# A two-layer graph network with fast matrix products: the statistics of u and h laid between the inner copies, adj's T4 and the logit weights moved in the first batch, and the first softmax's exponentials put to other steps

## The chip, the cores and the metric

The kernel runs on one core of a Trainium2 chip. The metric is the time of one execution on the device in microseconds (us), the median of several runs. A core has TensorE (PE, matrix products; PEld is its loading of weights), VectorE (DVE), ScalarE (ACT), GpSimd (POOL) and the queue SP, which here only issues transfers (DMAs). Each engine works through its own instructions in the order in which the program wrote them. [...]

## The reference

```python
# x: 16 x 1024 x 512, adj: 1024 x 1024, all float32
# layer 0
h = maximum(layernorm(x), 0)
x = x + (adj @ h) @ W0 + bias
# layer 1 (graph attention)
u = maximum(layernorm(x), 0)
hw = u @ W1
e = leaky_relu(s1[:, :, None] + s2[:, None, :], 0.2) * adj   # s1 = hw @ a1, s2 = hw @ a2
att = softmax(e, axis=2)
x = x + elu(att @ hw + beta * hw)
```

The kernel works out att @ u first and multiplies by W1 afterwards; beta is added on the diagonal of att. So s1 and s2 come straight from u: u times (W1 @ a1) and u times (W1 @ a2). These two vectors are the "logit weights".

## The kernel before

All 16 batches go through layer 0, and then all 16 through layer 1. Every large product is made with seven block products instead of eight (Strassen's scheme in Winograd's form). `PRODUCTS` (line 44) names them p1 to p7 with their two operands; S1 to S4 are sums of blocks of the left operand, T1 to T4 of the right one. `ReadA` (line 121) takes the finished products out of the accumulators (PSUM): ScalarE copies p1, p6, p5 and p4, VectorE adds p2, p7 and p3 and then makes the sums S1, S2, S3 for the product with W.

One batch of layer 0 has two parts. The first is adj times h ("y"). In batch 0 it is made by the plain `products_a` in 14 steps, in the others by `products_a2` (line 193) in 28 steps, k = 0 to 27. There four of the seven products (p1, p5, p3, p4) are themselves made with seven inner products, written in the order r1, r4, r5, r6, r2, r7, r3. Inner products alternate with quarters of the plain ones: p1 with p2 (steps 0 to 6), p5 with p6 (7 to 13), p3 with p7 (14 to 20), and p4 with the first product of the second part (21 to 27). Between inner products small copies and sums have to be made before the next may overwrite its accumulator: ScalarE copies r1, r5 and r7 into the tiles y_p1t, in_p (the sums' last quarter) and so on, VectorE adds to r6 (`step`, line 229). The operands' inner block sums are made ahead of that by `inner_left` (line 384). The second part is y times W0 ("po"), by `Weighted` (line 304), in 14 steps of two per product. Its results are added to the tiles xr, which hold x as the residual; GpSimd adds the bias to them (`add_bias`).

Between these steps everything else is laid by hand. A plan is a table of step numbers with functions that are called after the step; `beside` (line 520) calls them. Every engine's instructions and every transfer are kept in the order of writing (`InOrder`, line 103), which is also why each record of the profile has line 111. In batch b of layer 0 these stand beside the products:

- for batch b - 1, after its residual is complete: `keep` stores x + layer 0 for layer 1; `stats` are ScalarE's sums for the layer norm of u (a pass for the mean, one for the variance), `relu` makes u in place, `logits` multiplies it on VectorE with the two logit weights, `sums` makes u's block sums, `store` writes u away (`plan_out`, line 1071). `load_res` then loads the next residual into the same tiles. Full-size outputs that nobody needs, of `stats` and of `logits`, go into a half of the tile of S1 of u (`junk`, line 610), the half chosen by q.
- for batch b + 1: `h_stats` and `h_relu` make h out of x, `h_sums` its block sums (`plan_norm_a`, `plan_norm_b`, lines 1098 and 1105).
- for layer 1's first softmax, ahead of time: in batches 5 to 12 one eighth each of the masked logits e is made and stored (`EARLY_B`, line 1143); batch 15 reloads these (R), takes their exponentials with transposes (E), makes the sums over rows (S, s), the diagonal (D, d) and the block sums T1 to T3 (`FIRST_A`, `FIRST_B`, lines 1151 and 1155).

From batch 1 on, steps 0 and 1 of the second part's plan are called in the first part, after its steps 23 and 26 (line 1201).

In batch 0 `plan_first` (line 1051) also transposes adj, makes its block sums T1 to T4 and their inner sums, and the two logit weights are worked out in steps 3 and 5 of the second part.

Of the kernel before, what the change touches and what calls it, by code (L numbers as in the profile page):

```python
# [61 lines left out]
def kernel(  # L62
# [58 lines left out]
    class ReadA:  # L121
# [1 line left out]


        def __init__(self, name):
            self.name, self.c, self.s = name, {}, {}

        def block(self, n, p):
            if n not in self.c:
# [3 lines left out]
        def __call__(self, prod, p, ps):  # L133
            s = self.s
            if prod == "p1":
                act.copy(self.block("C11", p), ps)
            elif prod == "p2":
                c11 = self.block("C11", p)
                add(c11, ps, c11)
            elif prod == "p6":  # L140
                act.copy(self.block("C12", p), ps)
            elif prod == "p5":
                act.copy(self.block("C22", p), ps)
            elif prod == "p7":
                c22 = self.block("C22", p)
                add(c22, ps, c22)
            elif prod == "p3":
                if not s:
                    for k in ("S1", "S2", "S4"):
                        s[k] = b4.tile([P, 2, 512], F32, tag="b4", name=f"{self.name}_{k}")  # L150
                c11, c12, c22 = (self.block(n, p) for n in ("C11", "C12", "C22"))
                s1, s2 = s["S1"][:, p, :], s["S2"][:, p, :]
                add(c12, ps, c12)
                add(s1, c12, c22)
                add(s2, s1, c11, ALU.subtract)
                add(c12, c11, c12, ALU.subtract)
            else:
                act.copy(self.block("C21", p), ps)
                self.last(p)

        def last(self, p):
            add(self.s["S4"][:, p, :], self.block("C21", p), self.s["S2"][:, p, :], ALU.subtract)
# [30 lines left out]
    def products_a2(name, a_blk, b_blk, inner, weighted, after):  # L193


        read = ReadA(name)
        banks = {}
        by_name = {p[0]: (n, *p[1:]) for n, p in enumerate(PRODUCTS)}

# [74 lines left out]
        for two, one in (("p1", "p2"), ("p5", "p6"), ("p3", "p7")):  # L274
            inn, pla = inner_steps(two), plain_steps(one)
            for m in range(7):
                inn[m]()
                pla[m if m < 4 else m + 1]()
                if m == 3:
                    pla[4]()  # L280
                    if one != "p2":
                        reads(one, 0)
                elif m == 5:
                    reads(two, 0)
                    if one == "p2":
                        reads(one, 0)
                elif m == 6:
                    for prod in (two, one) if one == "p2" else (one, two):
                        reads(prod, 1)
                after(k + m)  # L290
            k += 7
        inn = inner_steps("p4")
        steps = iter(weighted.steps(0, read.c["C11"]))
        for m in range(7):
            inn[m]()
            if m > 4:
                read.last(m - 5)
            next(steps)()
            if m == 3:
                next(steps)()  # L300
            after(k + m)
        return read.left()

# [258 lines left out]
    def layer0_b(b, plan):  # L562
        left = lefts.pop(b)
        if b in weighted:
            weighted.pop(b).rest(1, left, beside(plan))
        else:
            Weighted(f"po{b}", w0_c, partial(to_residual, b)).rest(0, left, beside(plan))

    x1d = {}
    ud = {}  # L570
# [480 lines left out]
    def plan_first():  # L1051
        return {
            1: [(h_sums, 0, 0), (transpose_adj, 0, 1), (transpose_adj, 1, 0), (h_sums, 0, 1)]
            + [(transpose_adj, 1, 1), (adj_sum, "T1"), (adj_sum, "T2")],
            4: [(adj_sum, "T3")], 5: [(adj_sum, "T4")], 6: [(w_sums, w0_c)],
            7: [(inner_right, "p1", 0), (inner_right, "p1", 1)],
            8: [(inner_right, "p5", 0), (inner_right, "p5", 1)], 9: [(inner_right, "p3", 0)],
            10: [(inner_right, "p4", 0)],
        }
# [4 lines left out]
            plan.setdefault(k, []).append(tuple(step))  # L1064
        return plan

    def in_fourteen(plan):

        return merged(*({k // 2 if k > 0 else k: v} for k, v in plan.items()))

    def plan_out(o, b):

        return steps(
            (-1, o.keep, 0, 1), (-1, o.keep, 1, 0), (-1, o.keep, 1, 1), (-1, o.stats, 0, 1, 1),
            (0, o.stats, 1, 0, 0), (1, o.stats, 1, 0, 1), (2, o.stats, 1, 1, 0),
            (3, o.relu, 0, 0), (4, o.stats, 1, 1, 1), (5, o.relu, 1, 0), (6, o.relu, 0, 1),
            (8, o.relu, 1, 1),
            (0, inner_left, b, "p3"), (1, inner_left, b, "p4"),
            (5, o.logits, 0, 0, 0), (7, o.logits, 0, 0, 1),
            (8, o.logits, 1, 0, 0), (9, o.logits, 1, 0, 1),  # L1080
            (10, o.sums, 0, 0), (11, o.sums, 0, 1), (11, o.store, 0),
            (12, o.logits, 0, 1, 0), (13, o.logits, 0, 1, 1), (13, load_res, b, 0, 0),
            (14, o.logits, 1, 1, 0), (15, o.logits, 1, 1, 1), (15, load_res, b, 1, 0),
            (16, o.sums, 1, 0), (17, o.sums, 1, 1), (17, o.store, 1),
            (19, load_res, b, 0, 1), (21, load_res, b, 1, 1),
        )

    def plan_bias(b):
# [8 lines left out]

    def plan_norm_a(b):
        return steps(
            (9, h_stats, b, 0, 0), (10, h_stats, b, 0, 1), (12, h_stats, b, 1, 0),  # L1100
            (13, h_stats, b, 1, 1), (14, h_relu, b, 0), (15, load_x, b, 2), (16, h_relu, b, 1),
            (17, load_x, b, 3),
        )

    def plan_norm_b(b):
        plan = steps(
            (0, h_stats, b, 2, 0), (1, h_stats, b, 2, 1), (2, h_stats, b, 3, 0),
            (3, h_stats, b, 3, 1), (4, h_relu, b, 2), (6, h_relu, b, 3), (8, h_sums, b, 0),
            (10, h_sums, b, 1),
        )  # L1110
        if b + 1 < B:
            plan = merged(plan, steps((7, load_x, b + 1, 0), (7, load_x, b + 1, 1)))
        return merged(plan, steps((12, inner_left, b, "p1"), (13, inner_left, b, "p5")))

    def plan_softmax(order, s):
        names = {
# [12 lines left out]
        for n in ("T1", "T2", "T3", "T4"):  # L1129
# [13 lines left out]
    EARLY_B = {  # L1143
        4: {10: "L"},
        **{
            5 + g: {4: f"e{g}", 8: f"M{g}", 12: f"K{g}" + {3: " X", 7: " x"}.get(g, "")}
            for g in range(NCH)
        },
        13: {9: "N n"},
    }  # L1150
    FIRST_A = {
        1: "R0", 4: "R1", 7: "B E0 R2", 9: "E1 R3", 12: "E2 R4", 14: "E3", 15: "S b", 17: "R5",
        21: "R6", 22: "E4",
    }
    FIRST_B = {
        0: "E5", 1: "D R7", 2: "E6", 4: "E7 s", 7: "T1a", 8: "T1b", 10: "d", 11: "T2a",
        12: "T2b", 13: "T3a T3b",
    }
    LOADS_U = {5: ("U00",), 7: ("U01",), 9: ("U10", "U11"), 11: ("S2",), 13: ("S1", "S4")}


# [2 lines left out]
    for b in range(B):  # L1164
        plans = [plan_out(out_of, b)] if b else []
        plans_b = [plan_bias(b)]
        if b + 1 < B:
            plans.append(plan_norm_a(b + 1))
            out_of = LayerOut(b)
            plans_b += [  # L1170
                plan_norm_b(b + 1), plan_softmax(EARLY_B.get(b, {}), sms[0]),
                steps(
                    (11, out_of.stats, 0, 0, 0), (12, out_of.stats, 0, 0, 1),
                    (13, out_of.stats, 0, 1, 0), (12, out_of.keep, 0, 0),
                ),
            ]
        else:
            plans.append(plan_softmax(FIRST_A, sms[0]))
            plans.append({
                22: [(load_u, 0, ("U00", "U01"))], 25: [(load_u, 0, ("U10", "U11"))],  # L1180
            })
            plans_b += [
                plan_softmax(FIRST_B, sms[0]), plan_softmax(LOGITS_B, sms[1]),
                steps((3, load_u, 0, ("S2", "S1", "S4"))),
            ]
        if 0 < b <= G:
            plans.append({23: [(store_mask, b - 1)]})
        if b == 0:
            plan_b = merged(
                {  # L1190
                    1: [(inner_right, "p3", 1)], 2: [(inner_right, "p4", 1)],
                    3: [(logit_weights, 0)], 5: [(logit_weights, 1)],
                },
                *plans_b,
            )
            layer0_a(b, merged(plan_first(), in_fourteen(merged(*plans))))
        else:
            if b == 1:
                plans.append({-1: [(logit_weights_back, 0), (logit_weights_back, 1)]})
            plan_b = merged(*plans_b)  # L1200
            plans.append({k: plan_b.pop(i) for k, i in ((23, 0), (26, 1))})
            layer0_a2(b, merged(*plans))
        layer0_b(b, plan_b)


# [5 lines left out]
    for b in range(B):  # L1211
# [4 lines left out]
        plans.append({7 + i: [(load_x1, b, nh, q)] for i, (nh, q) in enumerate(halves)})  # L1216
        plan_b = {}
        if b == 0:
            plans.append({12: [(w_sums, w1_c)]})
        if b + 1 < B:  # L1220
            plans.append(plan_softmax(SOFTMAX_A, sms[b + 1]))
            plans.append({k: [(load_u, b + 1, n)] for k, n in LOADS_U.items()})
# [50 lines left out]
```

## Time and profile before

| | us |
|---|---|
| median of the runs (2347.12 to 2350.27) | 2349.37 |
| the profiled execution | 2345.13 |
| its span, first to last instruction | 2343.3 |
| PE, DVE, ACT, POOL busy | 2294.7, 1782.8, 1496.8, 582.9 |
| layer 0, batch 0 (from 11.0, the first instructions before it) | 87.5 |
| layer 0, batch 1 | 69.5 |
| layer 0, batch 7 | 71.1 |
| layer 0, batch 15 | 84.6 |
| layer 1, batch 0 | 72.2 |
| mean granted TensorE clock | 0.995 |

A row of the profile names the engine, the operation, the tile written and the tiles read without their numbers: y_p5t is batch b's small tile of p5, y_Y, y_X, y_W are accumulators of the first part, y_C its blocks read out, po_Y those of the second part; xr is the residual and later u; hS and in_p are sums of h; uS with s is the logits' output, uS with mv_u that of u's statistics; er is an eighth of e loaded back, and pT its transpose. "[1.15 <-ACT y_C]" behind a row means that the engine stood idle for 1.15 us before it, until ScalarE's writing of y_C released it. A batch's length is taken from the start of its p1 to the next.

### The profile page before, as it was taken

Reading aid. Unit: us, or ns where it says so; the run is one execution under the profiler, and the core shown is the slowest. Engines: PE = TensorE matmul, PEld = TensorE weight load, DVE = VectorE, ACT = ScalarE, POOL = GpSimd, SP = SyncE. Lnnn points to the kernel's source line nnn. Section 1 sums busy time; section 2 is a strip of 40 time slices with the busy share of each in tenths; the row PEclk is TensorE's granted clock in tenths of the full one; section 3 lists DMA queues with packets and bytes.
Section 4 is the critical chain, followed back from the end, with each engine's and each line's share of the span. In section 5 each row is a group of like instructions: output and inputs, shape, how many; then the busy total and the mean of one; then the engine's idle time right before and its main releaser. Section 6 shows DMA issues by size and latency. Waiting matters only on the chain.

```text
span 2343.3 us, 28480 instructions
## 1 busy us (share of the span) xinstructions
PE 2294.7 (98%) x7984; PEld 1511.0 (64%) x7984; DVE 1782.8 (76%) x3932; ACT 1496.8 (64%) x4025; POOL 582.9 (25%) x680
## 2 busy tenths in 40 slices
PE   9899999999999999999899999999999999999998
PEld 5677777777667777677655666556665566655665
DVE  4887777787777787877877787777877778777774
ACT  4565767665767666666357676666766677667743
POOL 1333223333223333232102221122211222102220
PEclk9999999999999999999999999999999999999999
DMA  6254544454543554433754556555565545555541
GB/s 229 64 189 153 171 151 131 153 189 145 171 150 124 168 189 145 163 120 123 245 184 155 166 178 206 173 178 166 189 211 173 186 159 167 179 182 166 175 128 44
DMA packets 207247, 383.15 MB, mean 164 GB/s; under 512 B 80240, under 2 KB 88432, under 8 KB 207088
## 3 DMA queue, kind: packets, MB, share of 16 engines
q1 hardware_dynamic: 206768, 380.81, 49.8%
q8 instruction: 63, 1.03, 0.2%
q14 instruction: 96, 0.79, 0.1%
q10 hardware_dynamic: 320, 0.52, 0.1%
HBM read 251.92 MB, written 133.50 MB: 164 GB/s over the span
## 4 chain that ended last, share of the span: by engine, by line
PE 60%; ACT 14%; DVE 13%; DMA 7%; issue 4%; SPq 2%; POOL 0%; ACTq 0%; DVEq 0%; POOLq 0%
PE z_Y L111 12%; PE y_Y L111 9%; PE pq_Y L111 6%; PE z_X L111 6%; PE po_Y L111 6%; ACT uS L111 5%; PE z_W L111 4%; PE pq_X L111 3%; PE y_X L111 3%; DVE e L111 2%; PE po_X L111 2%; DMA md<-mx 2%; ACT e L111 2%; PE po_W L111 2%; DVE hS L111 2%
## 5 line engine op out<-in xcount | busy, mean ns | idle before, releaser
L111 POOL TENSOR_TENSOR x<-x,r 128x512 f32<-128x512 f32 x120 | 226.0, 1894 | 874.7 <-DVE x L111 432.1
L111 ACT ACTIVATE e<-e,nm 128x256 f32<-128x256 f32 x480 | 237.4, 498 | 162.3 <-DVE nm L111 162.3
L111 DVE CUSTOM_DVE_ANT_0 e<-e,mask 128x256 f32<-128x256 f32 x512 | 233.2, 508 | 66.2 <-DMA mask<-maskd 34.8
L111 POOL TENSOR_TENSOR xr<-xr,bias_bc 128x512 f32<-128x512 f32 x128 | 168.2, 1336 | 269.0 <-DMA xr<-in_x_dram 182.8
L111 PE MATMUL z_Y<-pT,ul_U 128*128 128x512 f32 x512 | 224.9, 592 | 0.0
L111 ACT ACTIVATE e<-s2b,s1b 128x256 f32<-128x256 f32 x512 | 215.1, 506 | 9.0 <-DMA s2b<-s2d 9.0
L111 DVE STREAM_TRANSPOSE pT<-e 128x512 f32<-128x512 f32 x240 | 155.6, 686 | 67.4 <-ACT e L111 67.4
L111 PE MATMUL po_Y<-w_c,y_C 128*128 128x256 f32 x768 | 191.5, 384 | 3.8 <-DVE xr L111 3.8
L111 PE MATMUL pq_Y<-w_c,z_C 128*128 128x256 f32 x768 | 175.4, 380 | 0.6
L111 PEld LDWEIGHTS z_Y<-pT,ul_U 128*128 128x128 f32 x512 | 97.3, 190 | 115.6 <-issue 111.7
L111 DVE CUSTOM_DVE_ANT_0 uS<-xr,v_bc 128x512 f32<-128x512 f32 x240 | 165.7, 691 | 6.2
L111 ACT ACTIVATE r<-z,rs 128x256 f32<-128x256 f32 x192 | 95.7, 499 | 110.9 <-DVE z L111 110.9
L111 PEld LDWEIGHTS pq_Y<-w_c,z_C 128*128 128x128 f32 x768 | 145.1, 190 | 30.4 <-issue 7.7
L111 PEld LDWEIGHTS po_Y<-w_c,y_C 128*128 128x128 f32 x768 | 148.2, 193 | 25.5 <-DVE xr L111 4.2
L111 PE MATMUL y_Y<-adjT_B,h 128*128 128x512 f32 (+1 forms) x332 | 149.7, 554 | 1.6 <-ACT adjT_B L111 1.6
L111 ACT ACTIVATE uS<-xr 128x512 f32<-128x512 f32 x120 | 75.1, 626 | 119.0 <-DVE xr L111 102.7
L111 PE MATMUL y_Y<-adjT_T,hS 128*128 128x512 f32 x256 | 128.9, 599 | 9.8 <-ACT y_C L111 9.8
L111 PE MATMUL y_W<-adjT_B,h 128*128 128x512 f32 x256 | 127.2, 592 | 0.0
L111 ACT ACTIVATE h<-x,nb_h,r_h 128x512 f32<-128x512 f32 (+1 forms) x132 | 98.2, 793 | 44.6 <-POOL nb_h L111 43.4
L111 DVE TENSOR_TENSOR xr<-po_Y,xr 128x512 f32<-128x512 f32 x128 | 87.4, 684 | 41.6 <-PE po_Y L111 38.8
L111 ACT COPY z_C<-z_Y 128x512 f32<-128x512 f32 x96 | 55.5, 578 | 96.9 <-PE z_Y L111 96.9
L111 PE MATMUL po_X<-w_c,y_S 128*128 128x256 f32 x512 | 115.7, 379 | 0.0
(202 smaller groups left out, 4952.8 us busy)
## 6 DMA issues: line engine op xcount, KB each, us to landing
mask<-maskd SPq DMA_DIRECT2D x128, 512.0 KB
x<-in_x_dram SPq DMA_DIRECT2D x64, 512.0 KB
xr<-in_x_dram SPq DMA_DIRECT2D x256, 128.0 KB
x1d<-xr SPq DMA_DIRECT2D x64, 512.0 KB
ul_U<-ud_U SPq DMA_DIRECT2D x64, 512.0 KB
x<-x1d SPq DMA_DIRECT2D x64, 512.0 KB
out_dram<-x SPq DMA_DIRECT2D x252, 128.0 KB
ud_U<-xr SPq DMA_DIRECT2D x60, 512.0 KB
```

The lines of the kernel that those rows point to most:

```text
L111: return lambda *args, **kwargs: tc.keep_in_program_order(f(*args, **kwargs))
```

## The change

- Batch 0: T4 of adj is made after step 4 with T3, not after 5, and the logit weights after step 5 of the first part, not after 3 and 5 of the second; they are read back at step 0 of the second part, no longer at the start of batch 1. The plans that stand beside are no longer put to half their step numbers but to 4 plus half, at most 13. Its second part takes the order `A12_LATE`.
- Every later batch: a new order of `stats`, `relu`, `logits`, `sums`, stores and loads (`plan_out`); the h statistics and relus of batch b + 1 go from steps 9 to 16 to steps 14 to 19, and in the second part two steps later; `inner_left` of p5 goes into step 2 of the first part. The stats of u (0, 1, 0) are now made in the next batch.
- `products_a2`: both halves of p2 are read after step 7, no longer after 5 and 6. The sums S3 are made after p4's fourth inner product, not with p3's read.
- The early masks are loaded, used and stored at steps 0, 3 and 6 of the second part, no longer at 4, 8 and 12.
- Batch 15: the exponentials and reloads are at other steps, T3 is made in layer 1's first batch.

```diff
@@ class ReadA
-                add(c12, c11, c12, ALU.subtract)
+                if self.s3_now:
+                    self.s3(p)
...
+        def s3(self, p):
+            c11, c12 = self.block("C11", p), self.block("C12", p)
+            add(c12, c11, c12, ALU.subtract)
@@ products_a2
+        read.s3_now = False
...
-                if m == 3:
+                if m == 0 and two == "p5":
+                    reads("p2", 0)
+                    reads("p2", 1)
+                elif m == 3:
                     pla[4]()
                     if one != "p2":
                         reads(one, 0)
                 elif m == 5:
                     reads(two, 0)
-                    if one == "p2":
-                        reads(one, 0)
                 elif m == 6:
-                    for prod in (two, one) if one == "p2" else (one, two):
+                    for prod in (two,) if one == "p2" else (one, two):
                         reads(prod, 1)
...
             if m == 3:
                 next(steps)()
+                read.s3(0)
+                read.s3(1)
@@ layer0_b
-            Weighted(f"po{b}", w0_c, partial(to_residual, b)).rest(0, left, beside(plan))
+            Weighted(f"po{b}", w0_c, partial(to_residual, b), A12_LATE).rest(
+                0, left, beside(plan)
+            )
@@ plan_first
-            4: [(adj_sum, "T3")], 5: [(adj_sum, "T4")], 6: [(w_sums, w0_c)],
+            4: [(adj_sum, "T3"), (adj_sum, "T4")],
+            5: [(logit_weights, 0), (logit_weights, 1)], 6: [(w_sums, w0_c)],
@@
-    def in_fourteen(plan):
-
-        return merged(*({k // 2 if k > 0 else k: v} for k, v in plan.items()))
+    def at_end(plan):
+
+        return merged(*({min(4 + k // 2, 13): v} for k, v in plan.items()))
@@ plan_out
-            (-1, o.keep, 0, 1), (-1, o.keep, 1, 0), (-1, o.keep, 1, 1), (-1, o.stats, 0, 1, 1),
-            (0, o.stats, 1, 0, 0), (1, o.stats, 1, 0, 1), (2, o.stats, 1, 1, 0),
-            (3, o.relu, 0, 0), (4, o.stats, 1, 1, 1), (5, o.relu, 1, 0), (6, o.relu, 0, 1),
-            (8, o.relu, 1, 1),
-            (0, inner_left, b, "p3"), (1, inner_left, b, "p4"),
-            (5, o.logits, 0, 0, 0), (7, o.logits, 0, 0, 1),
-            (8, o.logits, 1, 0, 0), (9, o.logits, 1, 0, 1),
-            (10, o.sums, 0, 0), (11, o.sums, 0, 1), (11, o.store, 0),
-            (12, o.logits, 0, 1, 0), (13, o.logits, 0, 1, 1), (13, load_res, b, 0, 0),
-            (14, o.logits, 1, 1, 0), (15, o.logits, 1, 1, 1), (15, load_res, b, 1, 0),
-            (16, o.sums, 1, 0), (17, o.sums, 1, 1), (17, o.store, 1),
-            (19, load_res, b, 0, 1), (21, load_res, b, 1, 1),
+            (-1, o.keep, 0, 1), (-1, o.keep, 1, 0), (-1, o.keep, 1, 1), (0, o.stats, 0, 1, 0),
+            (1, o.stats, 0, 1, 1), (2, o.stats, 1, 0, 0), (3, o.stats, 1, 0, 1),
+            (4, o.relu, 0, 0), (7, o.relu, 0, 1), (8, o.stats, 1, 1, 0), (9, o.stats, 1, 1, 1),
+            (10, o.relu, 1, 0), (11, o.relu, 1, 1),
+            (0, inner_left, b, "p3"), (1, inner_left, b, "p4"), (2, inner_left, b, "p5"),
+            (5, o.logits, 0, 0, 0), (6, o.logits, 0, 0, 1), (8, o.logits, 0, 1, 0),
+            (9, o.logits, 0, 1, 1), (11, o.logits, 1, 0, 0), (12, o.logits, 1, 0, 1),
+            (13, o.sums, 0, 0), (14, o.sums, 0, 1), (14, o.store, 0), (15, o.logits, 1, 1, 0),
+            (16, o.logits, 1, 1, 1), (16, load_res, b, 0, 0), (17, load_res, b, 0, 1),
+            (17, o.sums, 1, 0), (18, o.sums, 1, 1), (18, o.store, 1),
+            (21, load_res, b, 1, 0), (22, load_res, b, 1, 1),
@@ plan_norm_a
-            (9, h_stats, b, 0, 0), (10, h_stats, b, 0, 1), (12, h_stats, b, 1, 0),
-            (13, h_stats, b, 1, 1), (14, h_relu, b, 0), (15, load_x, b, 2), (16, h_relu, b, 1),
-            (17, load_x, b, 3),
+            (14, h_stats, b, 0, 0), (15, h_stats, b, 0, 1), (16, h_stats, b, 1, 0),
+            (17, h_stats, b, 1, 1), (18, h_relu, b, 0), (19, load_x, b, 2), (19, h_relu, b, 1),
+            (20, load_x, b, 3),
@@ plan_norm_b
-            (0, h_stats, b, 2, 0), (1, h_stats, b, 2, 1), (2, h_stats, b, 3, 0),
-            (3, h_stats, b, 3, 1), (4, h_relu, b, 2), (6, h_relu, b, 3), (8, h_sums, b, 0),
-            (10, h_sums, b, 1),
+            (2, h_stats, b, 2, 0), (3, h_stats, b, 2, 1), (4, h_stats, b, 3, 0),
+            (5, h_stats, b, 3, 1), (6, h_relu, b, 2), (7, h_relu, b, 3), (8, h_sums, b, 0),
+            (10, h_sums, b, 1), (12, inner_left, b, "p1"),
         )
         if b + 1 < B:
-            plan = merged(plan, steps((7, load_x, b + 1, 0), (7, load_x, b + 1, 1)))
-        return merged(plan, steps((12, inner_left, b, "p1"), (13, inner_left, b, "p5")))
+            plan = merged(plan, steps((8, load_x, b + 1, 0), (8, load_x, b + 1, 1)))
+        return plan
@@ EARLY_B
-            5 + g: {4: f"e{g}", 8: f"M{g}", 12: f"K{g}" + {3: " X", 7: " x"}.get(g, "")}
+            5 + g: {0: f"e{g}", 3: f"M{g}", 6: f"K{g}" + {3: " X", 7: " x"}.get(g, "")}
@@ FIRST_A, FIRST_B
-        1: "R0", 4: "R1", 7: "B E0 R2", 9: "E1 R3", 12: "E2 R4", 14: "E3", 15: "S b", 17: "R5",
-        21: "R6", 22: "E4",
+        1: "R0", 4: "R1", 7: "B E0 R2", 10: "E1 R3", 12: "R4", 15: "E2", 18: "b R5", 22: "R6",
...
-        0: "E5", 1: "D R7", 2: "E6", 4: "E7 s", 7: "T1a", 8: "T1b", 10: "d", 11: "T2a",
-        12: "T2b", 13: "T3a T3b",
+        0: "E3 S", 1: "E4 R7", 3: "E5", 4: "E6", 6: "E7 s", 7: "D", 9: "T1a", 10: "T1b", 11: "d",
+        12: "T2a", 13: "T2b",
     }
+    FIRST_T3 = {2: "T3a", 3: "T3b"}
@@ the loop over layer 0, batch 0
+                    0: [(logit_weights_back, 0), (logit_weights_back, 1)],
                     1: [(inner_right, "p3", 1)], 2: [(inner_right, "p4", 1)],
-                    3: [(logit_weights, 0)], 5: [(logit_weights, 1)],
...
-            layer0_a(b, merged(plan_first(), in_fourteen(merged(*plans))))
+            layer0_a(b, merged(plan_first(), at_end(merged(*plans))))
```

More of the change, by code (lines that the diff above doesn't have):

```diff
@@ L125, in __init__ @@
         def __init__(self, name):
-            self.name, self.c, self.s = name, {}, {}
+            self.name, self.c, self.s, self.s3_now = name, {}, {}, True
         def block(self, n, p):
@@ L1172 @@
                 steps(
-                    (11, out_of.stats, 0, 0, 0), (12, out_of.stats, 0, 0, 1),
-                    (13, out_of.stats, 0, 1, 0), (12, out_of.keep, 0, 0),
+                    (11, out_of.stats, 0, 0, 0), (11, out_of.keep, 0, 0),
+                    (12, out_of.stats, 0, 0, 1),
                 ),
@@ L1195 @@
             )
-            layer0_a(b, merged(plan_first(), in_fourteen(merged(*plans))))
+            layer0_a(b, merged(plan_first(), at_end(merged(*plans))))
         else:
-            if b == 1:
-                plans.append({-1: [(logit_weights_back, 0), (logit_weights_back, 1)]})
             plan_b = merged(*plans_b)
@@ L1218 @@
         if b == 0:
-            plans.append({12: [(w_sums, w1_c)]})
+            plans += [{12: [(w_sums, w1_c)]}, plan_softmax(FIRST_T3, sms[b])]
         if b + 1 < B:
```

## The prediction

> **What bounds the kernel now.** I read the busy shares first, then what TensorE waits for, then a table of stretches cut at the batch starts, then the order of one batch on ScalarE beside TensorE.
>
> The busy shares of the page:
>
> ```profile
> PE 2294.7 (98%) x7984; PEld 1511.0 (64%) x7984; DVE 1782.8 (76%) x3932; ACT 1496.8 (64%) x4025; POOL 582.9 (25%) x680
> ```
>
> The waits of TensorE (us in total, times, longest):
>
> ```profile
> PE y_Y L111 <- ACT y_C L111: 9.8, 9, 1.2
> PE y_p4y L111 <- DVE y_p4t L111: 6.4, 1, 6.4
> PE y_p5y L111 <- ACT y_p5t L111: 5.9, 15, 0.4
> PE po_Y L111 <- DVE xr L111: 4.2, 2, 3.8
> PE y_p5y L111 <- DVE y_p5t L111: 3.1, 1, 3.1
> PE y_Y L111 <- DVE y_C L111: 1.4, 1, 1.4
> PE y_p3y L111 <- DVE y_p3t L111: 0.8, 1, 0.8
> ```
>
> TensorE is the bound: the change touches no matmul, so it can win only what TensorE loses between matmuls. The list says where: 15 and 8 short waits that recur with the batch, and a few long single ones. The stretches of batches 0, 1, 7, 15 and of layer 1's first (us from the span's start, length, busy time of PE, PEld, DVE, ACT, POOL, granted clock, DMA):
>
> ```profile
> 11.00:98.50 87.50, 81.53 (x273) 49.31 (x273) 62.66 (x97) 38.08 (x89) 21.18 (x30) 0.96 0.41 121
> 98.50:168.00 69.50, 69.16 (x273) 51.56 (x272) 53.03 (x108) 44.88 (x115) 21.45 (x33) 1.00 0.54 185
> 588.70:659.80 71.10, 69.55 (x274) 51.55 (x274) 54.34 (x117) 46.58 (x119) 21.77 (x33) 1.00 0.45 149
> 1085.30:1169.90 84.60, 73.87 (x274) 53.86 (x273) 64.22 (x134) 40.13 (x124) 15.07 (x21) 0.94 0.62 208
> 1169.90:1242.10 72.20, 72.20 (x225) 42.55 (x224) 54.34 (x137) 45.12 (x130) 7.00 (x4) 1.00 0.52 171
> ```
>
> Matmul records follow each other at 0.429 us (512 columns) and 0.216 us (256); counted out, a batch of layer 0 with inner products needs 69.05 us. Batches 1 to 5 take 69.6, 6 to 13 take 71.04, 14 takes 70.4, 15 takes 84.6. Layer 1 has no gap to give. ScalarE, then TensorE, in batch 7:
>
> ```profile
> 603.18 0.58 ACT L111 COPY y_C<-y_Y 128x512 f32<-128x512 f32 x1 [0.77 <-DVE y_Y L111]
> 603.67 1.52 ACT L111 ACTIVATE xr<-xr,nb_u,r_u 128x512 f32<-128x512 f32 x2
> 606.96 1.52 ACT L111 ACTIVATE xr<-xr,nb_u,r_u 128x512 f32<-128x512 f32 x2
> 608.38 0.35 ACT L111 COPY y_p5t<-y_p5y 128x256 f32<-128x256 f32 x1
> ```
>
> ```profile
> 603.82 1.13 PE L111 MATMUL y_Y<-adjT_T,hS 128*128 128x512 f32 x2 [1.15 <-ACT y_C L111]
> 608.79 1.13 PE L111 MATMUL y_p5y<-ext,in_p 128*128 128x256 f32 x4 [0.40 <-ACT y_p5t L111]
> ```
>
> The small copy y_p5t stands behind a relu on u, and p1's copy (y_C) comes late because a u statistic stands ahead of p1's inner copy. Start to start the gaps cost 1.3 and 0.56 us.
>
> **The change, part by part.**
>
> *Batch 0.* T4 of adj, now built beside T3 at step 4, finds a free buffer; before, VectorE stood 17.64 us (34.2 to 51.8) for one. The logit weights move from po's steps 3 and 5 to step 5 of the first half. Before, they ran at 78.5 to 88.7, and while GpSimd's bias adds ran their 128x512 operation took 1.62 us, alone 0.67; TensorE waited 3.80 us behind them and then ran at clock 0.50 for 6.8 us. Moved, the eight of them (8 x 0.72 = 5.8 us) fall at 36.4 to 42.2 with GpSimd idle, inside VectorE's former 17.64 us. Gain: 3.80, half of 6.8 = 3.4, the 1.38 us wait of p4 for y_C and about 0.4 of a second residual wait: 8.9. The h statistics of batch 1, put to steps 11 to 13, and two x loads behind their relus land at about 72 us and are needed at 80: nothing. The weights' read-back is two loads, needed a batch later.
>
> *Batches 1 to 14, old waits.* In the new order no u statistic or relu lies between p1's inner copy and its two y_C copies, and y_p5t follows these directly. Both waits above go: 0.56 in each batch; in 6 to 13 a further 1.99 - 0.56 = 1.43.
>
> *Batches 1 to 15, a new wait.* The u statistics (ScalarE) and the logits (VectorE) throw their unneeded full-size output into the same half of uS1, so the second pair's instructions alternate: logits(0,1,0) behind stats(1,1,0), stats(1,1,1) behind these logits, logits(0,1,1) behind that, and then VectorE's y_p5t sum, for which p5's product r7 waits. From the start of p1's r7 to that of p5's r7 TensorE has seven steps, 6 x 1.72 + 2.58 = 12.90 us. The chain, by rows of this trace: r7 1.07; copy 0.38; sum 0.61; logits 1.44; sum 0.73; y_C copy 0.49; y_p5t copy 0.26; relu 1.41; statistic 1.81; logits 1.48; statistic 1.86; logits 1.39; sum 0.42; start 0.06: 13.41. Late by 0.5 us. The chain has fourteen links and misses by a twenty-fifth of itself, so the cost is 0 to 1.2 us; I take 0.5. Queued behind it on VectorE are logits(1,0) and p5's large sums, with over 1 us to spare. Net: batches 1 to 5, 69.63 to 69.55, together -0.4; 6 to 13, 1.49 each, -11.9; 14, -0.8.
>
> *Edits hidden in all batches.* p2's read a step later delays only C11, used at p3. inner_left(p5), 4 x 0.34 us, goes to step 2; p5 starts at step 7. Statistics and relus of h (1.8 and 1.5 us) go to steps 14 to 19, where ScalarE, busy 46 of 71 us, loses the u work; in po they stand two steps later, and h's sums at steps 8 and 10 still find them. The stores and loads move on SP: the store at step 18 issues seven DMAs in about 6.4 us (as at 1128.3 to 1134.9), so the loads of xr(1,.) at 21 and 22 issue until about 43.5 us into the batch and land by 46; p5's residual add needs them at 3 x 12.90 + 9.5 (p4) + 1.7 = 49.9. Without those 4 us VectorE would hold po's banks, us for us. Mask loads, then masks and their stores stand earlier by four to six steps and fill po's idle ScalarE.
>
> *S3 behind p4's first inner sum.* Two 0.69 us adds leave the queue ahead of y_p4t and fill VectorE's 1.63 us idle after it. Here a rule speaks against: the Trainium skill, "SBUF — State Buffer", "Who interferes with whom", says that a VectorE instruction with two SBUF inputs and a GpSimd one that reads SBUF exclude each other for their whole length. A bias add (1.42 us) stands at step 23. The like add y_S<-y_C,y_S took 0.69 alone, 1.04 at 640.43 and at most 1.53 beside bias adds. By the rows two S3 adds take up to 3.06, 1.4 more than the idle time; by the rule up to 2 x (0.69 + 1.42) = 4.2, 2.6 more. VectorE next idles 1.10 and 1.03 us ahead of residual adds, TensorE has free banks there: 0 by both, with the rule 0.5 us a batch at the worst.
>
> *Batch 15.* Before: y_p4t late by 6.44 behind an exp that waited 5.71 for its reload, y_p5t by 3.06, y_p3t by 0.84, and clock about 0.5 for 6.8 and 3.4 us: 15.5 over 69.05. After: exp 0 (4 x 0.49 = 1.97 us) now stands in the chain above: 0.50 + 1.97 = 2.45 at p5's r7. Exp 2 delays p3: C22's copy 0.85, r7 0.65. Exp 3 with two transposes stands ahead of y_p4t: 1.2. Sum 5.2; reloads have three steps or more. The clock decides the rest:
>
> ```profile
> 88.00:90.00 2.00, 2.00 (x6) 1.53 (x6) 1.97 (x7) 0.00 (x0) 0.00 (x0) 0.50 0.10 1
> 1111.00:1113.00 2.00, 1.35 (x3) 1.17 (x4) 1.97 (x5) 0.58 (x1) 0.00 (x0) 0.57 0.01 4
> ```
>
> Gaps of 3.06, 3.80 and 6.44 us were each followed by a half clock, gaps of 1.2 never. The skill's "TensorE: Matmul & The Clock Gate", "Why this matters for your kernels", allows gaps to about 3 us, and its window of 3.4 us runs free. By its limit 2.45 us is safe, batch 15 takes 74.3 (-10.3); by the nearest row, 3.06 us with 3.4 us at half clock, 1.7 comes back (-8.6). Half-way: -9.5. The T3 sums, now in layer 1 (2 x 1.21 us), find VectorE at 54 of 72 us: nothing.
>
> *Sum.* -8.9 - 0.4 - 11.9 - 0.8 - 9.5 = -31.5. The profiled execution, 2345.1 (span 2343.3 and 1.8 around it), becomes 2313.6. The runs' median stands 4.2 above that execution; so 2318.
>
> **The rivals.**
>
> 1. *The alternating chain is longer* (each hand-over dearer, or ScalarE late at its start): 1.2 us a batch adds 15 x 0.7 = 10.5: 2328, up to 2345. For it: fourteen links without slack. Against it: each is a measured duration.
> 2. *No chain wait, batch 15 clean*: 15 x 0.5 + 3.5 less: 2307.
> 3. *Batch 15 pays again*: reloads held on SP behind stores, another 3 us gap and half clock: +8, 2326. For it: its 5.71 us wait before.
> 4. *The change doesn't do what it says in 6 to 13*: ScalarE's early relus wait for the store of x1d, and y_C stays late: +11.9, 2330. Against: those stores were issued 4 steps before.
> 5. *Slower.* At p5's r7 the chain wait passes the point where the clock falls, in every batch. It needs 31.5 / 15 = 2.1 us more a batch: 2.6 us of wait. With 3.06 us and 1.7 of clock, as at 1111, each batch costs 4.3 more: 15 x 4.3 = 64, 2382. For it: two engines bound to each other by a tile nobody reads. Against: the links would have to be wrong by a fifth.
>
> **How the numbers follow.** As worked 0.55 (own range 2310 to 2325); rival 1 0.13, 2 0.14, 3 0.08, 4 0.03, 5 0.07. Runs here differ by 0.13%, so 0.2%, 4.7 us, is what can be told from no change. Rival 1's tail gives 0.02 within it, rival 5's start 0.01: faster 0.91, same 0.03, slower 0.06. The range, 2303 to 2337, holds the likeliest and rivals 2, 3, 4 and most of 1.
>
> **What the profile after would show.** y_Y waiting for ACT y_C and y_p5y for ACT y_p5t gone from TensorE's waits; p1 of batch 1 starting at about 89.6 and no half clock before it; y_p5y waiting for DVE y_p5t some 15 times, 0.3 to 0.9 us each, with VectorE's logits waiting for ACT uS and ScalarE's uS for DVE s; batches 1 to 14 at 69.5 each; batch 15 at 74 to 76. The prediction is wrong if that new wait passes 1.2 us, if it is put elsewhere, or if batch 15 keeps a gap over 3 us.

## The result

The changed kernel takes 2329.66 us (median; 2329.23 to 2330.04) against 2348.24 for the kernel before (2344.18 to 2350.27): a ratio of 0.9923, interval 0.9906 to 0.9940. It is faster, by 18.6 us in the medians and by 15.1 in the profiled executions (2345.13 to 2330.04). 2318 was predicted, with 2303 to 2337 as the range: right in sign, and about half of the gain that was summed up, 31.5 us, is missing. The busy shares of the changed kernel's page, and what its TensorE waits for:

```profile
PE 2292.2 (98%) x7984; PEld 1511.3 (65%) x7984; DVE 1808.8 (78%) x3932; ACT 1503.0 (65%) x4025; POOL 586.5 (25%) x680
```

```profile
PE y_p5y L111 <- DVE y_p5t L111: 8.5, 15, 2.9
PE po_Y L111 <- DVE xr L111: 7.4, 3, 4.6
...
PE y_p4y L111 <- DVE y_p4t L111: 1.4, 1, 1.4
PE pq_Y L111 <- ACT z L111: 1.0, 2, 0.7
PE pq_Y L111 <- DVE z L111: 0.5, 1, 0.5
```

The two recurring waits for ScalarE are gone from the list, as forecast. In their place stands the forecast one, for VectorE's y_p5t, 15 times. Not forecast: 7.4 us for xr in three places, and the waits of pq_Y in layer 1 (z is att times u there, pq the product of that with W1). Batches 0, 1, 7, 10, 15 and layer 1's first (from and to, length, busy time of PE, PEld, DVE, ACT, POOL, granted clock, DMA share, GB/s):

```profile
11.20:89.80 78.60, 78.16 (x273) 47.78 (x274) 59.35 (x95) 37.40 (x86) 18.68 (x29) 1.00 0.49 156
89.80:159.20 69.40, 69.20 (x274) 51.58 (x273) 53.58 (x107) 44.36 (x112) 21.62 (x33) 1.00 0.48 160
576.70:646.70 70.00, 69.21 (x274) 51.58 (x273) 57.65 (x117) 47.25 (x120) 22.45 (x33) 1.00 0.49 161
716.40:790.60 74.20, 71.19 (x274) 52.68 (x273) 57.14 (x120) 48.40 (x124) 22.30 (x33) 0.98 0.45 153
1070.00:1151.90 81.90, 73.06 (x273) 53.41 (x272) 63.91 (x135) 41.05 (x128) 16.11 (x21) 0.96 0.58 195
1151.90:1225.80 73.90, 72.85 (x226) 42.45 (x226) 56.61 (x141) 45.61 (x132) 7.09 (x4) 1.00 0.57 193
```

The difference of the two spans, 15.0 us, by stretches cut at the starts of p1:

| stretch | forecast | measured |
|---|---|---|
| batch 0 | -8.9 | -8.7 |
| batches 1 to 5 | -0.4 | -0.8 |
| batches 6 to 13 | -11.9 | -5.1 |
| batch 14 | -0.8 | -0.8 |
| batch 15 | -9.5 | -2.6 |
| layer 1 | 0 | +2.9 |

So the question is where 6.8 us in batches 6 to 13, 6.9 in batch 15 and 3 in layer 1 went.

### The profile page after: what moved, and what is told of

It reads as the page before. It is cut to its first block, busy times and chain, and to the rows that moved or that the text cites. A ratio compares the mean times of both kernels' runs of the same rounds, so it can differ in the third digit from the quotient of the medians.

```text
span 2328.3 us, 28484 instructions
## 1 busy us (share of the span) xinstructions
PE 2292.2 (98%) x7984; PEld 1511.3 (65%) x7984; DVE 1808.8 (78%) x3932; ACT 1503.0 (65%) x4025; POOL 586.5 (25%) x680
## 4 chain that ended last, share of the span: by engine, by line
PE 41%; DVE 18%; ACT 17%; DMA 15%; issue 4%; SPq 3%; POOL 3%; DVEq 0%; ACTq 0%; POOLq 0%
PE z_Y L111 8%; PE y_Y L111 6%; PE pq_Y L111 4%; ACT e L111 4%; ACT uS L111 4%; PE po_Y L111 4%; PE z_X L111 4%; DVE e L111 3%; DMA md<-mx 3%; SPq L111 3%; DVE uS L111 3%; DMA x<-in_x_dram 3%; PE z_W L111 2%; DMA mask<-maskd 2%; PE pq_X L111 2%
## 5 line engine op out<-in xcount | busy, mean ns | idle before, releaser
L111 DVE CUSTOM_DVE_ANT_0 e<-e,mask 128x256 f32<-128x256 f32 x512 | 239.2, 519 | 73.1 <-DMA mask<-maskd 42.9
L111 PE MATMUL pq_X<-w_c,z_S 128*128 128x256 f32 x512 | 115.6, 379 | 0.0
L111 PE MATMUL z_W<-pT,ul_U 128*128 128x512 f32 x256 | 112.5, 592 | 0.0
```

Source lines behind the costliest of these rows:

```text
L111: return lambda *args, **kwargs: tc.keep_in_program_order(f(*args, **kwargs))
```

## The experiments

Each kernel ran beside the kernel before; ratios are to that. The changed kernel itself: 0.9923. In code cuts `...` stands for what is left out. R7 is the reload of the eighth e number 7; r7, in small letters, is an inner product.

### The statistics' and the logits' common tile

```diff
-        def junk(self, q):
+        def junk(self, q, n="S1"):
-            return self.s["S1"].rearrange(...)[:, ts(q, D)]
+            return self.s[n].rearrange(...)[:, ts(q, D)]
 def logits:
-  self.us[nh, q][:, k, :], self.junk(q), v_bcs
+  self.us[nh, q][:, k, :], self.junk(q, "S2"), v_bcs
```

> The changed kernel with one edit: the logits throw their unneeded output into the tile of S2 of u, the statistics theirs into S1 as before, so the two engines no longer alternate. My theory: the 15 waits of TensorE for VectorE's y_p5t (8.5 us idle, 10.9 with restarts) and their half clock in batch 15 (1.7) go, and as VectorE gets back the 3.4 us that it stands in each batch at this tile, the stores and the loads of xr(1,.) come earlier and the waits of batches 9 to 11 for xr (2.9, with restart and clock 4) go too: 2329.7 - 15 = 2315. Rival, the loads are late by SP's own order: only the first part goes, 2318 to 2320. Rival, the next limit stands right behind (ScalarE's in_p copy or the logits themselves): y_p5t still waits 0.2 or more in each batch, 2324 or more.

Measured: 2315.55 us, ratio 0.9862 (0.9848 to 0.9877). First what the wait looks like in the changed kernel, batch 9, VectorE and then ScalarE:

```profile
664.59 0.69 DVE L111 CUSTOM_DVE_ANT_0 uS<-xr,v_bc 128x512 f32<-128x512 f32 x1 [1.49 <-ACT uS L111]
...
667.89 0.69 DVE L111 CUSTOM_DVE_ANT_0 uS<-xr,v_bc 128x512 f32<-128x512 f32 x1 [1.87 <-ACT uS L111]
...
669.25 0.42 DVE L111 TENSOR_TENSOR y_p5t<-y_p5y,in_p 128x256 f32<-128x256 f32 x1
```

```profile
666.06 0.63 ACT L111 ACTIVATE uS<-xr 128x512 f32<-128x512 f32 x1 [1.24 <-DVE s L111]
```

Logits wait 1.49 us for the statistic, the next statistic 1.24 us for the logits, the next logits 1.87 for that, and y_p5t stands behind them. With another tile for the logits (batches 7, 10 and 15 of that kernel):

```profile
573.00:642.00 69.00, 69.00 (x274) 51.56 (x272) 56.35 (x115) 45.90 (x115) 21.42 (x33) 1.00 0.48 157
710.90:779.90 69.00, 69.00 (x274) 51.71 (x274) 57.26 (x117) 46.68 (x119) 21.06 (x33) 1.00 0.47 161
1056.20:1138.50 82.30, 74.88 (x273) 54.50 (x272) 65.29 (x138) 42.50 (x131) 15.21 (x21) 0.94 0.59 199
```

TensorE is busy in every microsecond of batches 7 and 10: the tile accounts for all that batches 1 to 14 lost, the wait of batch 10 for xr with it. In the changed kernel the loads of xr(1,.) were issued from 763.33 to 770.29 in batch 10, 46.9 to 53.9 us after its start; here from 755.06 to 760.39, 44.2 to 49.5. The store ahead of them waits for VectorE, which no longer stands the 3.4 us: it begins 36.1 us into the batch, not 38.5.

How much batch 10 lost is not set by its code alone. Four other kernels here (R7 first, R7 first with W1 late, T3 back, batch 0 undone) have the common tile and the same code in that batch; it took 70.2 to 71.9 us in them, not 74.2, with waits for xr of 0 to 1.7 us and no half clock.

In batch 15 of the kernel with two tiles the wait for y_p5t fell from 2.9 to 0.6, yet the batch takes 82.3: other waits (1.56, 1.96 and 3.33 us) hold it.

### Batch 15: the reload behind the sums

```diff
-        0: "E3 S", 1: "E4 R7", 3: "E5", ...
+        0: "R7 E3 S", 1: "E4", 3: "E5", ...
```

> The changed kernel with one edit in batch 15: the reload R7 is issued at step 0 of the second part ahead of E3 and the spreading of the sums S, not at step 1 behind them. Theory, the 4.57 us wait of po_Y for xr comes from SP: R7 stood behind S's read-back, which waited 5.7 us: R7 lands some 6 us sooner, exp 7 no longer holds VectorE, wait and half clock (4.7 + 1.7) go: 2323.5. Rival, the transfer itself is slow because all transfer engines are full with the loads of u (share 0.99): R7 lands at most 2 us sooner, 2327.

Measured: 2327.24, ratio 0.9912 (0.9895 to 0.9928): 1 to 3 us better, not 6. SP of the changed kernel (start, time over which it issued, transfer; sd are the sums written out, sall the same read back, er<-ed is R7):

```profile
1125.85 0.32 SPq L111 DMA_DIRECT2D sd<-sm  x1
1131.89 1.74 SPq L111 DMA_DIRECT2D sall<-sd  x4
1133.68 0.91 SPq L111 DMA_DIRECT2D ul_U<-ud_U  x2
1134.70 0.36 SPq L111 DMA_DIRECT2D er<-ed  x1
...
1142.56 0.32 SPq L111 DMA_DIRECT2D sd<-sm  x1
1144.36 1.75 SPq L111 DMA_DIRECT2D sall<-sd  x4
```

The read-back of the sums S waits from 1126.2 to 1131.9 for their store to land, and R7 behind it is issued at 1134.70. Store to read-back takes 6.0 us here, with a DMA share of 0.77; that of the second sums, s, takes 1.8 us, with a share of 0.37. Exp 7 began at 1140.46, its transposes at 1142.57 after 8.28 us of VectorE's idling, and po_Y's 4.57 us wait and a half clock followed. Moved, R7 is issued at 1127.02, exp 7 begins at 1134.03, and that wait is gone. Batch 15 and layer 1's first batch of this kernel:

```profile
1071.10:1145.80 74.70, 71.18 (x274) 52.41 (x273) 61.19 (x126) 39.66 (x122) 16.15 (x21) 0.98 0.59 205
1145.80:1227.60 81.80, 74.00 (x225) 41.95 (x224) 57.96 (x146) 45.48 (x132) 7.01 (x4) 1.00 0.52 179
```

81.9 became 74.7, as the theory says. But 73.9 became 81.8: the gain is given back one batch later. There VectorE stands 8.82 us for masks of the second softmax. The changed kernel has the like wait, 8.08 us; it ends 14.7 us into the batch there, and 22.9 us into it here. What moved is seen on SP of this kernel:

```profile
1138.59 0.39 SPq L111 DMA_DIRECT2D sd<-sm  x1
1145.75 2.67 SPq L111 DMA_DIRECT2D sall<-sd  x4
```

With the exps done sooner the second sums are stored sooner too, and from there to their read-back it takes 7.2 us instead of 1.8, with a DMA share of 0.79. The second softmax's inputs and masks stand behind it: the first masks are issued 6.5 us into the batch instead of 2.0 ahead of it.

> The changed kernel with R7 ahead of E3 and S in batch 15, and the load of W1 issued at step 3 of layer 1's first batch instead of before it. Reason: with R7 moved alone batch 15 took 74.7 us instead of 81.9, and layer 1's first batch 81.9 instead of 73.8. Theory, the second softmax's mask loads stand on SP behind the stores of x1 and the 5 us of W1's load, and their lateness took the gain back: without W1 ahead they come 5 us sooner, that batch falls to 74 to 77, the whole to 2320 to 2322. Rival, the masks are slow for want of buffers and bandwidth: that batch stays at 80 or more, 2327.

```diff
-    w1_c = load_w("w1_c", w1)        # ahead of layer 1
+    {3: [(load_w1,)], 12: [(lambda: w_sums(w1_c),)]}   # step 3 of its first batch
```

Measured, R7 first and W1 late: 2324.27, ratio 0.9897 (0.9870 to 0.9925); batch 15 took 74.7 us, layer 1's first batch 78.3. So the queue in front of the masks is a part of it, some 3.5 us; about 4.5 us remain, of which 2.0 and 1.7 are waits for ScalarE's copies in pq. The second read-back comes after 7.0 us in this kernel too, and is the likely cause of the rest; no run moves it alone.

### T3 of the first softmax

```diff
-        12: "T2a", 13: "T2b",
-    FIRST_T3 = {2: "T3a", 3: "T3b"}
+        12: "T2a", 13: "T2b T3a T3b",
+    FIRST_T3 = {}
```

> The changed kernel with T3 of the first softmax back at step 13 of batch 15's second part (as in the kernel before). Theory, its two sums in layer 1's first batch made VectorE late in pq (waits of 0.68 and 0.37 us for z): that batch falls from 73.8 to 72.3 us, the whole by 1.5. Rival, the sums now fall between batch 15's last residual adds and the first reads of z and cost the same there: 0.

Measured: 2327.46, ratio 0.9914 (0.9900 to 0.9929). Layer 1's first batch took 73.1, against 73.9 in the changed kernel, but 72.7 with the tile alone, where T3 stands as changed. It is 72.2 in the kernel before. The place of T3 is worth between 0 and 0.8 us here; this run doesn't settle it. The next 14 batches of layer 1, whose code is the same in all these kernels, lose together 4.7 to 11.9 us to waits from one profile to the next (7.7 before, 8.9 changed): 1.2 of the 2.9 us are of that kind.

### Batch 0

```diff
-            4: [(adj_sum, "T3")], 5: [(adj_sum, "T4")], 6: ...
+            4: [(adj_sum, "T3"), (adj_sum, "T4")],
+            5: [(logit_weights, 0), (logit_weights, 1)], 6: ...
-        return merged(*({k // 2 if k > 0 else k: v} ...))
+        return merged(*({min(7 + k // 2, 13): v} ...))
-            Weighted(f"po{b}", w0_c, partial(to_residual, b)).rest(0, ...)
+            Weighted(f"po{b}", w0_c, partial(to_residual, b), A12_LATE).rest(0, ...)
+                    0: [(logit_weights_back, 0), (logit_weights_back, 1)],
-                    3: [(logit_weights, 0)], 5: [(logit_weights, 1)],
```

> The kernel before with the edits of batch 0 alone (T4 with T3, logit weights at step 5 of the first part, read back at step 0 of the second, plans at the end of the fourteen, order A12_LATE). Theory: p1 of batch 1 starts at 89.8 instead of 98.5, all else as before: -8.7, 2339.5. Rival, the start is taken back in batch 1 by loads that land late: -5 or less.

The 7 stands for the change's 4, since the old plan's steps for h are lower. Measured: 2343.01, ratio 0.9983 (0.9973 to 0.9993): 3 to 4 us instead of 8.7. p1 of batch 1 starts at 93.1, and batch 1 takes 72.0. VectorE of this kernel:

```profile
84.06 0.69 DVE L111 TENSOR_TENSOR xr<-po_W,xr 128x512 f32<-128x512 f32 x1 [7.44 <-POOL xr L111]
```

It stands for GpSimd's bias adds; these stand behind the h statistics, which stand behind x loads that the plan now issues last.

The next kernel has these edits and a second one, in `plan_norm_b`:

```diff
-            (0, h_stats, b, 2, 0), ... (4, h_relu, b, 2), (6, h_relu, b, 3),
+            (2, h_stats, b, 2, 0), ... (6, h_relu, b, 2), (7, h_relu, b, 3),
```

> The kernel before with the edits of batch 0 and, in every batch, the h statistics and relus of the second part two steps later (steps 2 to 7), as in the change. Reason: with the edits of batch 0 alone VectorE stood 7.44 us for GpSimd's bias adds, which stand behind the h statistics, and these for x loads that the moved plan issues at the end. Theory, the two edits need each other: the bias adds go ahead, p1 of batch 1 starts at 90 (93.1 without), batch 1 takes 69.7 (72.0 without): 8 to 9 us below the kernel before. Rival, the late x loads are the cause: 3 below, as without it.

Measured: 2350.14, ratio 1.0012 (1.0003 to 1.0021): slower than the kernel before. p1 of batch 1 does start at 90.5, but batch 1 takes 72.4 and each of batches 2 to 14 0.4 to 1.2 us more than in the kernel before. The list of waits of this kernel:

```profile
PE y_Y L111 <- ACT y_C L111: 15.3, 15, 1.3
...
PE y_p1y L111 <- ACT y_p1t L111: 3.5, 6, 0.9
```

By the rows, with no run of its own: the bias adds now come later, an h block sum took 1.47 us beside them (at 508.49; 0.68 in the kernel before), the residual was ready later, and in the old order the u statistics, begun later, stand ahead of p1's inner copies. The last kernel undoes batch 0 in the changed kernel:

> The changed kernel with batch 0 as in the kernel before (T4 after step 5, logit weights at steps 3 and 5 of the second part, plans at half their steps, the plain order, read back at batch 1). Theory, batch 0's edits are worth 8.7 us in the company of the others: p1 of batch 1 at 98.5, all else as changed: 2329.7 + 8.7 = 2338. Rival, the h statistics now two steps later free VectorE of the bias adds in batch 0 by themselves: +4 to +5, 2334.

```diff
-            4: [(adj_sum, "T3"), (adj_sum, "T4")],
-            5: [(logit_weights, 0), (logit_weights, 1)], 6: ...
+            4: [(adj_sum, "T3")], 5: [(adj_sum, "T4")], 6: ...
-        return merged(*({min(4 + k // 2, 13): v} ...))
+        return merged(*({k // 2 if k > 0 else k: v} ...))
-            Weighted(..., A12_LATE).rest(0, ...)
+            Weighted(...).rest(0, ...)
-                    0: [(logit_weights_back, 0), (logit_weights_back, 1)],
+                    3: [(logit_weights, 0)], 5: [(logit_weights, 1)],
+                plans.append({-1: [(logit_weights_back, 0), (logit_weights_back, 1)]})  # b == 1
```

Measured: 2333.76, ratio 0.9940 (0.9924 to 0.9956): +4.1 in the medians, as the rival says. Its batch 0 is as short as with the edits:

```profile
11.20:90.20 79.00, 78.20 (x272) 47.68 (x273) 62.72 (x93) 36.17 (x82) 23.06 (x29) 1.00 0.45 132
90.20:163.60 73.40, 70.83 (x273) 52.52 (x272) 55.33 (x110) 46.15 (x118) 21.25 (x33) 0.98 0.52 176
```

Only batch 1 is longer, by 4.0: p5's r7 waits 2.57 us for y_p5t there, and the clock falls to half. What of the change still acts in batch 0 here is nearly all the new plan of h (statistics and relus later, and what moved with them). So this plan takes the wait and the half clock out of batch 0, with the logit weights still in po: GpSimd's bias adds end at 80.5 instead of 84.2 us. VectorE's 17.64 us for a buffer of T4 are gone too, though T4 stands after step 5 again. What the edits of batch 0 are worth they save in batch 1.

### S3

```diff
-        read.s3_now = False
...
-                read.s3(0)
-                read.s3(1)
```

> The changed kernel with the sums S3 made with p3's read again, ahead of p4's first inner sum. Theory, both places are hidden: no wait of TensorE for y_p4t in batches 1 to 14 and the same batch times, 0 (within 2 us). Rival, the place was worth something: y_p4y waits for VectorE in each batch, up to +0.5 us a batch, +7.

Measured: 2335.02, ratio 0.9947 (0.9927 to 0.9966). The rival holds:

```profile
PE y_p4y L111 <- DVE y_p4t L111: 14.4, 15, 2.6
```

0.82 us of waiting in most of the batches, which take 70.5 us instead of 69.4 to 70.0. Batches 1 to 14 together take 7.8 us more, batch 10 less (70.4 us instead of 74.2), since it has no wait for xr in this profile; the whole is 5.4 us slower in the medians. The kernel before had S3 there too and no such wait.

### Together

The tile, R7 and W1 in one kernel, and then two exponentials moved besides (the diff shows these alone):

> The changed kernel with its own tile for the logits' output, R7 ahead of E3 and S, and W1's load at step 3 of layer 1's first batch. Theory, the gains add: batches 1 to 14 at 68.95, batch 15 at 75 instead of 82.3, layer 1's first batch 74 to 76: 2309 to 2311. Rival, what batch 15 gains is taken back in layer 1: 2315, as with the tile alone.

```diff
-        7: "B E0 R2", 10: "E1 R3", 12: "R4", 15: "E2", ...
-        0: "R7 E3 S", 1: "E4", ...
+        7: "B E0 R2", 10: "R3", 12: "R4", 13: "E1", 15: "E2", ...
+        0: "R7", 1: "E3 S E4", ...
```

> The changed kernel with its own tile for the logits' output, R7 first, W1 late, and two exponentials of batch 15 moved: E1 from step 10 to 13 (behind p5's last copies of C22) and E3 from step 0 to step 1 of the second part (behind p4's last inner sum). Theory, the two waits left in batch 15 (y_X for ScalarE's y_C 1.56 us, y_p4y for VectorE's y_p4t 1.96 us with a clock drop) come from these two: they go, batch 15 falls from 75.0 to 71 us, the whole to 2310. Rival, the later exponentials make S and T1 late for layer 1's first batch, which takes it back: 2314.

Measured: 2313.78, ratio 0.9855 (0.9836 to 0.9875), and 2313.23, ratio 0.9856 (0.9834 to 0.9879). Both beat the changed kernel; neither can be told from the tile alone (0.9862). The first batch of layer 1 takes back half or more of what batch 15 gives: 75.0 and 76.7 us for the two in the first, 73.0 and 79.0 in the second, against 82.3 and 72.7 with the tile alone.

## Why the prediction was right, and where it was not

**The number**: closer than the working. On the profiled executions 2313.6 was forecast and 2330.0 measured, less than half of the gain. 2318 had 4.2 us added, by which the first three runs of the kernel before stood above its profiled execution; those of the changed kernel stand 0.4 below theirs. That is luck.

**The old waits go**: right. No y_Y or y_p5y of the inner products waits for y_C or y_p5t of ScalarE any more. The new order of u's statistics was not undone by itself, so this is read from the two lists. Counted out, a batch needs 68.95, not 69.05.

**The new wait**: right in mechanism and place. The chain was put at 0.5 us late, with 0 to 1.2 as bounds; the starts were late by 0.36 to 0.95 us in batches 1 to 14 (mean 0.57) and by 3.1 in batch 15, where 2.45 was forecast. What the step left out is VectorE's own standing in that chain, 3.4 us a batch. It was priced only by TensorE's wait.

**"The loads of xr(1,.) issue until about 43.5 us into the batch and land by 46"**: this step failed, and with it about 5 of the 6.8 us missing in batches 6 to 13 (batch 10 is 4.5 us longer than its neighbour, batch 11 by 0.75 of wait). The sum took SP's times from the plan's steps, which put the store of step 18 at 33 us. In batch 10 VectorE was three steps behind the plan at that point, so the store began at 38.5 us and the last load was issued at 53.9. VectorE in batch 10:

```profile
772.19 0.69 DVE L111 TENSOR_TENSOR xr<-po_X,xr 128x512 f32<-128x512 f32 x1 [3.90 <-DMA xr<-in_x_dram]
```

The first experiment shows what the common tile adds: with a tile for each the wait is gone. But the time itself was wrong without the tile too: there the store begins at 36.1 us and the last load is issued at 49.5, 6 us after the forecast. The kernel before had told it: its store of step 17 began 36.3 us into each of these batches. And the size is not the tile's alone, as the four kernels with the same code in batch 10 show. Of the rest, 1.3 is the chain's wait above 0.5.

**Batch 15, "reloads have three steps or more"**: failed. R7 is asked for at step 1 and used at step 6, but on SP it stands behind the read-back of S, which the change moved from the first part to step 0, and that waited 5.7 us, in whose first 4 us the DMA share was 0.99 to 1.02. The term of the sum was 0; it measured 4.7 us from start to start and a half clock. So rival 3, held at 0.08, came true here, behind a read-back where it said stores, and with 6.4 us of its 8; and one of the prediction's own signs of being wrong stood: batch 15 kept a gap over 3 us. The other terms: p5's r7 3.1 for 2.45, p4's r7 1.5 for 1.2, p3's two, 1.5 together, not seen. Even so half or more of the gain would not have stayed: four kernels with R7 first show it given back in layer 1. That the first softmax's end and the second's inputs share one queue is shown for W1's 3.5 us and read from SP's rows for the rest.

**The clock**: a gap of 2.9 us in batch 15 and one of 2.29 in batch 10 were followed by half clock, which the table's 0.96 and 0.98 show. So of the two values weighed, the row's was the right one, and the limit of about 3 us in the Trainium skill's "TensorE: Matmul & The Clock Gate", "Why this matters for your kernels", was not. Not by a rule, though: with T3 back, the gap in the same place was 2.17 us and the clock stayed whole.

**Batch 0**: the size was right (-8.7 for -8.9), its cause was not, so the agreement is luck. The step credited the moves of T4 and of the logit weights; in the changed kernel the new plan of h gives the same without them. One term was also read too large: of the 6.8 us at half clock 1.7 fell into the gap itself. Put into the kernel before, batch 0's edits gave less than half, and with the later h statistics beside them nothing. What was priced as independent terms is one arrangement.

**S3 at nothing**: the forecast of no wait held, but the cover was named too narrowly. VectorE's 1.63 us of idling were read in the old order; in the new one S3 ahead of y_p4t makes p4's inner product start 1.0 us late, and the move is what keeps that away.

**T3 at nothing**: the first batch of layer 1 is 1.6 longer than before; how much of it is T3 stays open between 0 and 0.8. The places of p2's read, of inner_left(p5) and of the early masks were not tried singly.

## What to carry to other kernels

A tile that only catches unneeded output still orders whoever writes it: two engines that throw into one tile wait for each other, and a second tile was worth more here than half of the whole change. A wait between two side engines is to be priced by all that stands behind it on both, down to the queue that their results feed, not by the first wait of the bound engine. And when many steps are re-laid together, test each edit in both directions, added to the old kernel and taken from the new: here the later plan of h shortened batch 0 without batch 0's own edits in the new order, and later h statistics cost some 7 us in the old one (ratio 0.9983 to 1.0012). A reload that is moved out of a queue's way lets what followed it come sooner as well, so look at what that meets.

## What the hardware showed that was not expected

The granted clock fell after shorter gaps than forecast, but not always. In the kernel with another tile for the logits a gap of 1.96 us before 1106.9 was followed by a clock of 0.59:

```profile
1106.90:1108.90 2.00, 2.00 (x6) 1.62 (x7) 1.71 (x3) 0.29 (x2) 0.00 (x0) 0.59 1.06 223
```

while in the kernel with R7 first a gap of 2.36 us before 1182.8, in layer 1, left it whole:

```profile
1182.80:1184.80 2.00, 1.96 (x5) 1.01 (x6) 2.00 (x4) 2.00 (x6) 0.00 (x0) 1.00 0.87 350
```

In all twelve traces, from the gap ahead of batch 0's first product to the last matmul, no gap of up to 1.79 us was followed by half clock, and each of 2.57 us or more was. From 1.84 to 2.37 us the length does not decide; 1.97 us with T3 back, in the same place as the 1.96 above, left it whole. Each such stretch of half clock lasted 3.4 or 6.8 us.

The time from the sums' store to its read-back followed the transfer load: in the changed kernel 1.8 us with a DMA share of 0.37 and 6.0 with 0.77. And a VectorE sum of two tiles took 1.47 and up to 1.77 us instead of 0.68 where a GpSimd bias add ran beside it, which moved the h block sums in one arrangement and not in another.
